# Two-layer graph network on one core: the first aggregation as seven products of 256 cubed, and the bias work moved behind the branch

## The chip, the cores and the metric

The kernel runs on one core of one Trainium2 chip. The metric is the device time of one execution in microseconds (us), from the first instruction to the last; runs of before and after are compared on the same chip. Five engines work in parallel, each through its own queue in order: PE (TensorE, matmuls), DVE (VectorE), ACT (ScalarE), POOL (GpSimd) and SP (which only issues DMAs).

## What is computed

The input x has 32 batches of 512 rows and 512 columns in fp32; adj is one 512 x 512 matrix for all of them. In short:

```python
h = relu(layernorm(x))
x = x + (adj @ h) @ W0 + b0                      # layer 0, per batch
h = relu(layernorm(x))
q, k, v = h @ Wq + bq, h @ Wk + bk, h @ Wv + bv   # 8 heads of 64
s = q @ k.T / 8 + (1 - adj) * -1e9
x = x + softmax(s) @ v @ Wo + bo                  # layer 1
```

The mask term has the size of 1e9 times a difference of adj, so a row's softmax puts all its weight on the column where adj has the row's maximum, as long as the scores are small against the gap. Then attention is a gather of rows: layer 1 becomes x + rows of (h @ Wv @ Wo + bv @ Wo + bo), and only those rows have to be computed that some row points to.

## The kernel before, in words

The function `gnn_two_layers` has two parts: work ahead of a branch (lines 72 to 308), and the branch (L310 on), which picks one of three paths by a number computed on the chip, the flag. On this input the path taken is `single_path` with room for 336 rows (its products are 168 wide).

**Ahead of the branch.** Everything stands in an order written out by hand, with no scheduler, so a line's place is its place in its engine's queue. The steps, in this order:

- Loads on SP and ACT (L88 to L97): Wv, Wo, adj, x of batch 0, Wq, Wk, W0, x of batch 1.
- Wv is transposed on PE (`turn`), and Wvo = Wv @ Wo is formed by `fold` (L149) in seven products of 256 cubed (Strassen's scheme in Winograd's form). Three PSUM banks `mm0` to `mm2` take the products; ACT copies or DVE adds them into `wvo`. The operand sums are made by `sum_a` and `sum_b` (L324 to L345), one DVE instruction each.
- The LayerNorm of batch 0 in two halves of two 128-row chunks (`norms[0]`, `norms[1]`). A half has four steps: `stats` (DVE, L359 and L360), `power` (DVE L365 and POOL L366), `offset` (DVE L369) and `relu` (ACT L377). The class `NormAct` does the same with statistics on ACT (L389; two passes with a running sum) and its own small steps at L397, L398 and L401.
- `peaks` (L156, L157): for each chunk of adj the row's eight largest values and the mask of the largest. `transposed` makes adjT on PE and copies it on ACT (L118).
- Five loads issued by POOL (L198, L200): bv, bq, bk as columns, b0 and bo as rows.
- The aggregation adj @ h of batch 0 (L270), as four groups of four 512-wide matmuls. Between them stand small products: the counts of used columns (L261, L264), the squared norms of Wq, bq, Wk, bk (L265, from ACT's `squares`, L240 and L241), the bias row bv @ Wo (L267, from the four `bias_part`s of DVE, L161 and L163) and the decision (L269).
- `decide` (L244 to L253) compares the least gap between a row's two largest values with a bound on the scores. L292 writes the flag.
- While PE finishes: two sums of Wvo, the addition of b0 to batch 0 (L298), the ReLU of batch 1, the index of each row's maximum (L304) and the bias column `cvo_c` (L305 and L308).

**Behind the branch.** `single_path` walks over the batches. In each round PE gets the layer 0 of batch b, the aggregation of batch b + 1, and the layer 1 of batch b - 1 (for b = 0: `layer0_rows`, L577, four groups of four 512-wide matmuls, and the aggregation of batch 1). Each of the three is a `product` of seven pieces of four matmuls (L451), with three to four PSUM banks taking turns; its pieces are p1, p5, u2, c11, c22, c12, c21. After each piece its bank is read by `take` (L488, L490, L498, L501, L508): c22, u2 and c21 continue in the bank of p1, c12 in that of p5, so a product that is added onto a bank waits for the read before it. All else is hung between the pieces: `put(batch, step, f)` puts a function into one of 21 steps of a round, steps 0 to 6 with the first product, 7 to 13 with the second and 14 to 20 with the third; in a step the functions come in the order of their `put`s, ahead of the `take`. In round 0, steps 3 to 6 are joined.

In round 0 the statistics of batch 0's second LayerNorm and of batch 2's first run on ACT (`NormAct`, eight pairs of L389). Steps 12 and 13 hold the remaining sums of W0 (L343, L345) and of Wvo (L331, L333).

Of the kernel before, what the change touches and what calls it, by code (L numbers as in the profile page):

```python
# [8 lines left out]
F32 = mybir.dt.float32  # L9
# [3 lines left out]
ALU = mybir.AluOpType  # L13
# [4 lines left out]
P = 128  # L18
HD = 64
EPS = 1e-5  # L20
NEG = 1e9
# [4 lines left out]
def gnn_two_layers(ctx: ExitStack, tc: tile.TileContext, x, adj, w0, b0, wq, bq, wk, bk, wv, bv, wo, bo, out):  # L26
# [22 lines left out]
    def big(name):  # L49
# [10 lines left out]
    before = keep.tile([P, C + 1], F32, name="before")  # L60
    idx = keep.tile([P, C, 8], U32, name="idx")
# [5 lines left out]
                wvo_t=wvo_t, cvo=cvo, cvo_c=cvo_c, b0_r=b0_r, used=used, before=before, idx=idx, ident=ident, ones=ones, mhalf=mhalf)  # L67
# [4 lines left out]
    with ExitStack() as tmp, tc.manual_schedule():  # L72
# [4 lines left out]
        part = look.tile([P, D], F32, name="part")  # L77
        wt = [look.tile([P, DC, D], F32, name=f"wt{i}") for i in range(2)]
        bt = [look.tile([P, DC], F32, name=f"bt{i}") for i in range(2)]
        bv_c = look.tile([P, DC], F32, name="bv_c")  # L80
# [71 lines left out]
        norms = [Norm(nc, small, mhalf, xs[0], hs[0], [0, 1]), Norm(nc, small, mhalf, xs[0], hs[0], [2, 3])]  # L152
# [5 lines left out]

        def bias_part(j):
            if j == 0:  # L160
                nc.vector.tensor_scalar_mul(part, wo_s[:, 0, :], bv_c[:, 0:1])  # L161
            else:
                nc.vector.scalar_tensor_tensor(part, wo_s[:, j, :], bv_c[:, j:j + 1], part, op0=ALU.mult, op1=ALU.add)  # L163
# [22 lines left out]
        nc.scalar.copy(blk(wvo, 1, 1), v)  # L186
        fold(u, wvT_t[:, 1], wo_t[:, 1], False)
        nc.scalar.copy(blk(wvo, 0, 1), u)
        peaks(0)
# [3 lines left out]
        norms[1].stats(0)  # L193
        norms[0].offset()
        norms[1].stats(1)
        norms[1].power()
# [6 lines left out]
        fold(u, wvT_t[:, 2], wo_t[:, 2], False)  # L203
        peaks(1)
        norms[1].offset()
        nc.vector.tensor_add(blk(wvo, 1, 1), u, blk(wvo, 1, 1))
# [3 lines left out]
        norms[0].relu(0)  # L210
        norms[0].relu(1)
        peaks(2)
        nc.vector.tensor_add(blk(wvo, 0, 1), v, blk(wvo, 0, 1))
        fold(u, blk(wvT, 1, 1), wo_t[:, 3], False)
        nc.scalar.copy(blk(wvo, 1, 0), u)
        norms[1].relu(0)
        norms[1].relu(1)
        peaks(3)

        both = look.tile([P, N], F32, name="both")  # L220
        nc.vector.tensor_add(both, sel[:, 0, :], sel[:, 1, :])
        for c in range(2, C):
            nc.vector.tensor_add(both, both, sel[:, c, :])  # L223

        tops = look.tile([P, C, 2], F32, name="tops")
        nc.vector.tensor_scalar(tops, top[:, :, 0:2], 1.0, NEG, op0=ALU.subtract, op1=ALU.mult)
        gap = look.tile([P, C], F32, name="gap")
        nc.vector.tensor_sub(gap, tops[:, :, 0], tops[:, :, 1])
        least = look.tile([P, 1], F32, name="least")
        nc.vector.tensor_reduce(least, gap, AX.X, ALU.min)  # L230
        for j in range(DC):
            bias_part(j)
# [22 lines left out]
        bias = corner(0).rearrange("p c q -> p (c q)")  # L255
        for d in range(DC):
            ps = bank((2, 1, 0, 2)[d]).rearrange("p a n -> p (a n)")
            for m in range(C):
                if d == 1 and m == 2:
                    for i in range(C):  # L260
                        nc.tensor.matmul(few[:, 0, i:i + 1], both[:, i * P:(i + 1) * P], ones[:, 0:1],  # L261
                                         start=True, stop=True)
                if d == 2 and m == 1:
                    nc.tensor.matmul(many[:, 0, :], ones, used, start=True, stop=True)  # L264
                    nc.tensor.matmul(many[:, 1, :], ones, sums, start=True, stop=True)  # L265
                if d == 2 and m == 3:
                    nc.tensor.matmul(bias, ones, part, start=True, stop=True)  # L267
                if d == 3 and m == 1:
                    nc.tensor.matmul(few[0:1, 1, 0:1], sure, ones[:, 0:1], start=True, stop=True)  # L269
                nc.tensor.matmul(ps, hs[0][:, m, d * P:(d + 1) * P], adjT[:, m, :], start=(m == 0), stop=(m == C - 1))  # L270
            if d == 0:
                squares(0)
            nc.scalar.copy(yT[:, d, :], ps)
            if d == 0:
                squares(1)
                for i in range(4):
                    sum_b(nc, adjT_s, adjT, i)
            if d == 1:
                nc.vector.tensor_scalar_min(used, few[:, 0, :], 1.0)
                if B > 1:  # L280
                    norms.append(NormAct(nc, small, mhalf, xs[1], hs[1], range(C)))
                    for c in range(C):
                        norms[2].stats(c)
                for i in range(2):
                    sum_b(nc, w0_t, w0_s, i)
            if d == 2:
                decide()
                nc.vector.memset(before[:, 0:1], 0.0)
                for m in range(1, C + 1):
                    nc.vector.tensor_add(before[:, m:m + 1], before[:, m - 1:m], many[:, 0, m - 1:m])  # L290
                nc.vector.tensor_add(cvo, bias, cvo)
        nc.vector.tensor_copy(flag, few[0:1, 1, 0:1])  # L292
        for i in range(2):
            sum_a(nc, wvo_t, wvo, i)
        if B > 1:
            norms[2].power()
# [755 lines left out]
```

## Time and profile before

| | us |
|---|---|
| time, median of 3 runs | 1081.98 (1081.93 to 1082.1) |
| the profiled execution's own time | 1081.54 |
| its span, first to last instruction | 1079.7 |
| PE busy | 1066.3 (99% of the span) |
| DVE busy | 898.7 (83%) |
| POOL busy | 447.1 (41%) |
| ACT busy | 376.2 (35%) |
| first aggregation, first matmul of L270 | 22.92 |
| flag written (L292) | 37.20 |
| first matmul behind the branch (L577) | 40.51 |
| first matmul of layer 0 of batch 1 | 67.98 |

The profile names an instruction by the line of the kernel it was issued from, the engine, the operation and "out<-in" by the names of the tiles. An fp32 matmul shows as two records. In a timeline a row is: start in us from the span's start, duration, engine, line, operation; in brackets the idle time of that engine ahead of it and who released it. In the chain that ended last, each piece was released by the one before it. The granted clock of PE was 0.999 throughout.

### The profile page before, as it was taken

How to read it: one execution, taken by the hardware profiler on the slowest of the kernel's cores; microseconds unless marked ns; L12 is line 12 of the kernel's file. 1: busy time of each engine (PE TensorE's matmuls, PEld its weight loads, DVE VectorE, ACT ScalarE, POOL GpSimd, SP SyncE). 2: the span in 40 equal slices, each digit the busy share in tenths (PEclk: the TensorE clock that was granted, in tenths of full speed). 3: DMA queues.
4: the chain of work that ended last, by engine and by line, in shares of the span. 5: the costliest groups of instructions: out<-in, count | busy, mean ns of one | idle time of the engine just before them, and what ended most of it. 6: DMA issues, size and time to landing. Idle time of an engine off the chain costs nothing.

```text
span 1079.7 us, 16014 instructions
## 1 busy us (share of the span) xinstructions
PE 1066.3 (99%) x5448; PEld 946.2 (88%) x5448; DVE 898.7 (83%) x1837; ACT 376.2 (35%) x709; POOL 447.1 (41%) x522
## 2 busy tenths in 40 slices
PE   9999999999999999999999999999999999999996
PEld 7478989999998999988999988999998999998993
DVE  6868888888888888888888888888888888888874
ACT  4744323334422324322323432323432323432331
POOL 2024554343554343554343454443454434355413
PEclk9999999999999999999999999999999999999999
DMA  9154666657776666767666767666776666766538
GB/s 330 40 92 145 183 184 160 157 169 197 186 185 158 165 168 187 193 174 183 148 169 184 199 170 195 143 168 175 205 187 183 148 157 180 199 180 165 133 106 272
DMA packets 162700, 186.92 MB, mean 173 GB/s; under 512 B 15024, under 2 KB 102832, under 8 KB 162608
## 3 DMA queue, kind: packets, MB, share of 16 engines
q1 hardware_dynamic: 132592, 116.73, 36.8%
q0 software_dynamic: 27968, 66.61, 27.4%
q10 hardware_dynamic: 2048, 2.46, 0.7%
q8 instruction: 45, 0.74, 0.3%
q14 instruction: 47, 0.39, 0.1%
HBM read 96.28 MB, written 89.46 MB: 172 GB/s over the span
## 4 chain that ended last, share of the span: by engine, by line
PE 93%; DVE 3%; DMA 2%; issue 1%; POOL 1%; ACTq 0%; ACT 0%; POOLq 0%; DVEq 0%
PE mm L451 91%; PE mm L577 1%; DMA x<-in_L_gnn_Wv_dram 1%; PE mm L270 1%; DMA yT<-z,place 1%; DMA z<-hc 0%; POOL hs L589 0%; DVE top L156 0%; DVE part L163 0%; DVE hc L656 0%; DVE st L359 0%; POOL rstd L398 0%; DVE sel L157 0%; DVE both L223 0%; POOL yT L674 0%
## 5 line engine op out<-in xcount | busy, mean ns | idle before, releaser
L665 POOL DMA_INDIRECT x<-z,place x116 | 182.8, 1576 | 351.3 <-issue 194.3
L490 ACT COPY yT<-mm 128x512 f32<-128x512 f32 x124 | 71.9, 580 | 541.9 <-PE mm L451 538.8
L508 DVE TENSOR_TENSOR x<-mm,x 128x512 f32<-128x512 f32 x217 | 149.8, 690 | 86.9 <-PE mm L451 86.9
L377 ACT ACTIVATE h<-x,off,rstd 128x512 f32<-128x512 f32 x256 | 194.5, 807 | 39.9 <-DVE off L369 35.8
L366 POOL TENSOR_TENSOR rstd<-ve,mhalf 128x2 f32<-128x2 f32 (+1 forms) x93 | 102.5, 1102 | 200.0 <-DVE ve L365 200.0
L451 PE MATMUL mm<-w_t,sel 128*128 128x256 f32 x744 | 171.0, 379 | 1.2 <-DVE x L508 1.2
L451 PE MATMUL mm<-adjT_s,h0s 128*128 128x256 f32 x744 | 171.0, 379 | 0.9 <-ACT yT L490 0.9
L359 DVE BATCH_NORM_STATS2 st<-x 128x6 f32<-128x512 f32 x244 | 163.4, 670 | 1.1
L451 PEld LDWEIGHTS mm<-w_t,sel 128*128 128x128 f32 x744 | 141.2, 190 | 20.8 <-DVE x L508 1.6
L451 PEld LDWEIGHTS mm<-adjT_s,h0s 128*128 128x128 f32 x744 | 141.2, 190 | 20.6 <-ACT yT L490 1.5
L589 POOL DMA_INDIRECT hs<-h,dest x124 | 133.2, 1074 | 23.6 <-issue 22.4
L451 PE MATMUL mm<-w_s,yT 128*128 128x256 f32 x496 | 117.2, 379 | 0.0
L451 PE MATMUL mm<-adjT,h 128*128 128x256 f32 x496 | 117.2, 379 | 0.0
L451 PE MATMUL mm<-hTs,wvo_t 128*128 128x168 f32 x720 | 112.4, 306 | 0.0
L501 ACT ACTIVATE zs<-mm,cvo_c 128x168 f32<-128x168 f32 x240 | 83.1, 397 | 75.0 <-PE mm L451 75.0
L451 PEld LDWEIGHTS mm<-adjT,h 128*128 128x128 f32 x496 | 94.2, 190 | 13.2 <-ACT h L389 0.2
L451 PEld LDWEIGHTS mm<-hTs,wvo_t 128*128 128x128 f32 x720 | 105.5, 190 | 0.0
L451 PEld LDWEIGHTS mm<-w_s,yT 128*128 128x128 f32 x496 | 92.9, 190 | 11.3
L557 DVE TENSOR_TENSOR x<-x,b_r 128x512 f32<-128x512 f32 x124 | 84.0, 677 | 0.0
L451 PE MATMUL mm<-hT,wvo 128*128 128x168 f32 x480 | 78.2, 306 | 0.0
L451 PEld LDWEIGHTS mm<-hT,wvo 128*128 128x128 f32 x480 | 72.7, 190 | 1.6
L488 DVE TENSOR_TENSOR yT<-mm,yT 128x512 f32<-128x512 f32 x93 | 64.0, 688 | 9.4 <-PE mm L451 4.9
(181 smaller groups left out, 1313.3 us busy)
## 6 DMA issues: line engine op xcount, KB each, us to landing
out_dram<-x SPq DMA_DIRECT2D x124, 256.0 KB, 4.7
x<-in_x_dram SPq DMA_DIRECT2D x120, 256.0 KB, 4.9
hc<-hs SPq DMA_DIRECT2D x124, 176.0 KB, 3.1
z<-zr SPq DMA_DIRECT2D x120, 96.0 KB, 2.0
z<-zr SPq DMA_DIRECT2D x120, 80.0 KB, 1.9
hs<-h,dest POOLq DMA_INDIRECT x124, 6.0
x<-z,place POOLq DMA_INDIRECT x116, 5.8
adj_s<-in_adj_dram SPq DMA_DIRECT2D x2, 512.0 KB, 5.8
```

Of the source, the lines that this page charges most:

```text
L270: nc.tensor.matmul(ps, hs[0][:, m, d * P:(d + 1) * P], adjT[:, m, :], start=(m == 0), stop=(m == C - 1))
L359: self.nc.vector.bn_stats(st, self.src[:, self.chunks[i], :])
L366: self.nc.gpsimd.tensor_tensor(self.rstd, ve, self.mhalf[:, 0:n], ALU.pow)
L377: self.nc.scalar.activation(dst, src, AF.Relu, bias=self.off[:, i:i + 1], scale=self.rstd[:, i:i + 1])
L451: nc.tensor.matmul(bank[:, m, 0:half], lhs[:, k, m * P:(m + 1) * P], rhs[:, k, :], start=(first and m == 0 and k == 0), stop=(k == 1), ski ...
L488: nc.vector.tensor_add(dst, bank, dst)
L490: nc.scalar.copy(dst, bank)
L501: nc.scalar.activation(dst[:, m, :], bank[:, m, :], AF.Identity, bias=cvo_c[:, 2 * i + m:2 * i + m + 1])
L508: nc.vector.tensor_add(dst, bank, dst)
L557: nc.vector.tensor_add(X[b][:, c, :], X[b][:, c, :], b0_r)
L589: stored = nc.gpsimd.indirect_dma_start(out=HS[b], out_offset=bass.IndirectOffsetOnAxis(ap=dest[:, i:i + 1], axis=0), in_=H1[b][:, i, :], ...
L665: nc.gpsimd.indirect_dma_start(out=X[b][:, c, :], out_offset=None, in_=Z[b], in_offset=bass.IndirectOffsetOnAxis(ap=place[:, c:c + 1], axi ...
```

## The change

- The aggregation of batch 0 ahead of the branch is done by a new helper `gemm` in seven products of 256 cubed, like all later ones. It needs four sums of h (`sum_a` into `wvT_t`, which is free by then) and four sums of adjT (`sum_b`, in the kernel before made between the groups). Three of the products are added to yT by DVE, four copied by ACT.
- The statistics of chunks 2 and 3 of batch 0 go to ACT (`NormAct`), and the order of powers, offsets, ReLUs, peaks and POOL's loads is changed with them.
- The bias row goes behind the branch: its parts to steps 9 and 10 of round 0, its product and addition to step 12. The bias column goes to step 6 of round 1.
- The sums of W0 (2 and 3) go from step 12 to step 8 of round 0, those of Wvo (2 and 3) from step 13 of round 0 to steps 5 and 6 of round 1. The sums 0 and 1 of W0 go behind the flag.
- In round 0 the second half of batch 0's second LayerNorm has its statistics on DVE, not on ACT.
- The small products of the decision stand behind the fifth, sixth and seventh product; L290's additions stand ahead of the flag as before.

```diff
-        norms = [Norm(nc, small, mhalf, xs[0], hs[0], [0, 1]), Norm(nc, small, mhalf, xs[0], hs[0], [2, 3])]
+        norms = [kind(nc, small, mhalf, xs[0], hs[0], [i, i + 1]) for i, kind in ((0, Norm), (2, NormAct))]
...
         nc.scalar.copy(blk(wvo, 1, 1), v)
+        norms[1].stats(0)
         fold(u, wvT_t[:, 1], wo_t[:, 1], False)
         nc.scalar.copy(blk(wvo, 0, 1), u)
+        norms[1].stats(1)
         peaks(0)
         for n in (0, 1):
             norms[0].stats(n)
         norms[0].power()
-        norms[1].stats(0)
-        norms[0].offset()
-        norms[1].stats(1)
-        norms[1].power()
         for t, d in ((bv_c, bv), (bt[0], bq), (bt[1], bk)):
             nc.gpsimd.dma_start(t, d.rearrange("(c p) -> p c", p=P))
...
         fold(u, wvT_t[:, 2], wo_t[:, 2], False)
+        norms[0].offset()
+        nc.vector.tensor_add(blk(wvo, 1, 1), u, blk(wvo, 1, 1))
+        norms[1].power()
         peaks(1)
         norms[1].offset()
-        nc.vector.tensor_add(blk(wvo, 1, 1), u, blk(wvo, 1, 1))
+        norms[0].relu(0)
+        norms[0].relu(1)
         next(flips)
         next(flips)
         fold(v, wvT_t[:, 3], wo_blk(1, 1), False)
-        norms[0].relu(0)
-        norms[0].relu(1)
+        norms[1].relu(0)
+        norms[1].relu(1)
         peaks(2)
+        for i in (0, 1):
+            sum_b(nc, adjT_s, adjT, i)
         nc.vector.tensor_add(blk(wvo, 0, 1), v, blk(wvo, 0, 1))
...
+        gemm(u, blk(h, 0, 0), blk(adjT, 0, 0), True)
+        squares(0)
+        nc.scalar.copy(blk(yT, 0, 0), u)
+        squares(1)
+        for i in (0, 1):
+            sum_a(nc, h_t, h, i)
+        gemm(w, blk(h, 1, 0), blk(adjT, 1, 0), True)
+        sum_a(nc, h_t, h, 2)
+        sum_b(nc, adjT_s, adjT, 2)
+        nc.vector.tensor_add(blk(yT, 0, 0), w, blk(yT, 0, 0))
+        gemm(u, h_t[:, 1], adjT_s[:, 1], False)
+        nc.scalar.copy(blk(yT, 0, 1), u)
+        peaks(3)
+        gemm(v, h_t[:, 0], adjT_s[:, 0], True)
+        nc.scalar.copy(blk(yT, 1, 1), v)
+        if B > 1:
+            norms.append(NormAct(nc, small, mhalf, xs[1], hs[1], range(C)))
+            for c in range(C - 1):
+                norms[2].stats(c)
...
+        gemm(u, h_t[:, 2], adjT_s[:, 2], False)
+        for i in range(C):
+            nc.tensor.matmul(few[:, 0, i:i + 1], both[:, i * P:(i + 1) * P], ones[:, 0:1], start=True, stop=True)
...
+        gemm(v, h_t[:, 3], blk(adjT, 1, 1), False)
+        nc.tensor.matmul(many[:, 0, :], ones, used, start=True, stop=True)
+        nc.tensor.matmul(many[:, 1, :], ones, sums, start=True, stop=True)
+        decide()
+        nc.vector.tensor_add(blk(yT, 0, 1), v, blk(yT, 0, 1))
+        gemm(u, blk(h, 1, 1), adjT_s[:, 3], False)
+        nc.tensor.matmul(few[0:1, 1, 0:1], sure, ones[:, 0:1], start=True, stop=True)
+        nc.scalar.copy(blk(yT, 1, 0), u)
+        if B > 1:
+            norms[2].stats(C - 1)
+        nc.vector.memset(before[:, 0:1], 0.0)
+        for m in range(1, C + 1):
+            nc.vector.tensor_add(before[:, m:m + 1], before[:, m - 1:m], many[:, 0, m - 1:m])
         nc.vector.tensor_copy(flag, few[0:1, 1, 0:1])
         for i in range(2):
             sum_a(nc, wvo_t, wvo, i)
+        for i in range(2):
+            sum_b(nc, w0_t, w0_s, i)
...
-                halves = [norm(X[b], H1[b], [2 * i, 2 * i + 1], Norm if b > 0 else NormAct) for i in range(2)]
+                halves = [norm(X[b], H1[b], [2 * i, 2 * i + 1], Norm if b > 0 or i == 1 else NormAct) for i in range(2)]
...
                 for i in (2, 3):
-                    put(0, 12, lambda b, i: sum_b(nc, w0_t, w0_s, i), i)
-                    put(0, 13, lambda b, i: sum_a(nc, wvo_t, wvo, i), i)
+                    put(0, 8, lambda b, i: sum_b(nc, w0_t, w0_s, i), i)
+                for j in range(DC):
+                    put(0, 9 + j // 2, lambda b, j: bias_part(j), j)
+                put(0, 12, lambda b: bias_row())
...
+                for i in (2, 3):
+                    put(1, 3 + i, lambda b, i: sum_a(nc, wvo_t, wvo, i), i)
+                put(1, 6, lambda b: bias_column())
```

The removed lines of the old aggregation are L255 to L291 of the kernel before; the functions `bias_part`, `bias_row` and `bias_column` have the instructions of L161, L163, L267, L291, L305 and L308, unchanged.

## The prediction

> **What bounds the kernel now.** I read the page first: TensorE is busy 99% of the span and the chain that ended last lies on it for 93%.
>
> ```profile
> span 1079.7 us, 16014 instructions
> ...
> PE   1066.3 (99%) x5448; PEld 946.2 (88%) x5448; DVE 898.7 (83%) x1837; ACT 376.2 (35%) x709; POOL 447.1 (41%) x522
> ...
> PE 93%; DVE 3%; DMA 2%; issue 1%; POOL 1%; ACTq 0%; ACT 0%; POOLq 0%; DVEq 0%
> ```
>
> Second came the chain in order of time: from 100.89 us on it is one unbroken piece of PE, 953.68 us long, so the change can only act in the first 101 us and in what they hand on. Third, the timeline of PE up to there (start, time, what, and in brackets the idle time before it with its releaser):
>
> ```profile
> 22.92 5.31 PE L270 MATMUL mm<-adjT,h 128*128 128x512 f32 x12
> ...
> 34.16 1.02 PE L267 MATMUL pt<-part,ones 128*128 128x512 f32 x2
> ...
> 40.51 7.10 PE L577 MATMUL mm<-w_s,yT 128*128 128x512 f32 x16 [0.72 <-ACT yT L273]
> ...
> 59.24 1.99 PE L451 MATMUL mm<-adjT_s,h0s 128*128 128x256 f32 x8 [0.86 <-ACT yT L490]
> ...
> 62.80 1.89 PE L451 MATMUL mm<-adjT_s,h0s 128*128 128x256 f32 x8
> 64.52 1.89 PE L451 MATMUL mm<-adjT,h0s 128*128 128x256 f32 x8
> ...
> 72.79 1.99 PE L451 MATMUL mm<-w_t,sel 128*128 128x256 f32 x8 [1.20 <-DVE x L508]
> ```
>
> The last rows give the price of a product of 256 cubed: 64.52 - 62.80 = 1.72 us. The 16 records of L577 take 6.94 us until L525 starts, so a 512-wide matmul is two records, 0.87 us. Fourth, the timelines of DVE, POOL and SP, for the steps that move:
>
> ```profile
> 37.05 0.15 DVE L292 CAST flag<-few 1x1 int32<-1x1 f32 x1 [1.14 <-PE few L269]
> ...
> 43.75 0.67 DVE L305 TENSOR_TENSOR part<-cvo,ident 128x512 f32<-128x512 f32 x1
> 44.45 0.69 DVE L308 TENSOR_REDUCE cvo_c<-part 128x4 f32<-128x512 f32 x1
> ...
> 80.73 0.70 DVE L359 BATCH_NORM_STATS2 st<-x 128x6 f32<-128x512 f32 x1
> ...
> 100.34 0.49 DVE L498 TENSOR_TENSOR zs<-mm,zs 128x336 f32<-128x336 f32 x1
> ```
>
> From 80.73 to 100.83 DVE idles only 1.4 us (0.81 waiting for POOL's power, 0.17 and 0.42 for PE). At 100.89 PE waits for that L498. So there DVE, not PE, hands the time on.
>
> [...] the trace has 0.68 to 0.69 us, and such instructions follow each other every 0.60 us, which I use. [...] the flag is written at 37.20, SP's first DMA behind the branch starts at 37.92, 0.72 us. [...]
>
> **The change, part by part.** I laid out each engine's queue in its new order, with durations from the rows above and each instruction behind what it reads.
>
> *Ahead of the aggregation.* The statistics of chunks 2 and 3 of batch 0 go from DVE to ACT, two pairs of 1.46 us (from the L389 rows). One pair now stands before the copy of the second folding bank, so the next fold waits about 0.35 us at 16.2; but the addition into wvo now stands ahead of the peaks on DVE and PE's 0.36 us wait at 21.09 is gone. Nil: the aggregation starts at 22.9 as before. Moved past POOL's five loads: the second power. They take 3.63 us (19.99 to 23.62), started now at 18.0, so the power is done at 22.4. Behind it DVE has the offset, one pair of peaks (1.14), two adjT sums (1.3) and the addition that empties a folding bank: 25.7. The second product writes that bank and is ready at 24.6, so PE waits 1.1 us, a new wait. Its bounds are 0 (if the power were served between the loads) and 1.1. And if the small loads bq and bk land later than 5.6 us after issue (they now run beside the big loads), the squares on ACT hold the copy of the first product and up to 1 us more is lost. I take zero for that.
>
> *The aggregation.* Removed: 16 matmuls of 0.863 = 13.8 us. Added: 28 of 0.432 = 12.1 us. The bias matmul (0.86) leaves. The count products (0.80 + 0.44 + 0.11) stay. From 22.9: 12.1 + 1.35 + 1.1 = 37.4 us as PE's end, against 39.8 before. The operand sums (seven more DVE instructions, 4.2 us) are costed at nothing: four bias parts (2.7), the bias addition (0.6) and two bn_stats pairs (1.6) leave DVE's queue there, 4.9 us. If they didn't cover it, each sum in front of its product would cost its 0.60. But now the flag comes last: the decision waits for products behind the sixth of seven, and a yT addition, the memset and four dependent additions of 0.20 stand before the flag's cast. It ends at 38.45, 1.25 us later than before, and PE has nothing queued. With SP's 0.72 us PE restarts at 39.15 instead of 40.51: lead 1.36 us. Bounds of this restart: 0.35 us (DVE's own gap at the branch, 45.14 to 45.48) and 3.3 us (all that the old row could have hidden, 37.20 to 40.51).
>
> *Behind the branch to the first wait.* Layer 0 of batch 0 and two products are equal in both: PE is ready for the third at 56.8. DVE does the same amount between flag and branch (two w0 sums for the bias column) but starts 1.2 us later, so ACT's statistics start at 47.9, not 46.93. ACT has six pairs instead of eight: 8.8 + copy 0.6, done at 57.25. PE waits 0.45, restarting at 57.3 against 59.24: lead 1.94. The bias matmul comes back (0.86), waiting for nothing since its four parts end at about 61.7: lead 1.1 at 66.8.
>
> *The 1.20 us wait at 72.79.* DVE had two w0 sums and two wvo sums in front of the four sums of yT and the first addition of x. All four are moved away. From the bias product (ends 65.1) DVE needs 0.7 + 0.65 + 2.7 + 0.7 to that addition, 69.8; PE needs it at 70.25. The wait is gone and the lead is 2.5 us. Slack 0.4.
>
> *The giving back.* One wvo sum and the bias column have been put behind the statistics of batch 1: 0.60 + 0.70 + 0.65 = 1.95 us more in the saturated stretch of DVE that begins at 80.73. It begins 2.5 us earlier, but ends only 2.5 - 1.95 + 0.59 (its two waits for PE, which vanish) = 1.15 us earlier. PE, ahead by 2.5, waits for DVE and ACT at about 86, 90 and 99 us, 1.3 us in all. Behind 101 us PE has no wait to lose, and loads, stores and gathers move along with it.
>
> *Sum.* The profiled execution: 1079.7 + 1.84 around the span = 1081.54 us; minus 1.15 gives 1080.4. The runs' median is 1081.98, so 1080.8 on that footing.
>
> **Rivals.** A difference under 0.2% (2.2 us) is about what a measurement of this kernel can tell from none.
>
> *Nothing is given back.* The 2.5 us stay: 1079.5, faster. For it: PE is the 99% engine. Against it: the L498 row and DVE's density from 80 to 101. It would need the three instructions to fall into idle time, of which there is 0.8 us.
>
> *The exposed branch decides: slower.* In the new order every engine learns the path only when PE is empty. If PE's restart takes 3.3 us instead of 0.72, 2.6 us are lost, of which the 0.45 us wait at 57 takes up some: 1080.8 + 2.1 = 1082.9. Slower than before from a restart of about 2.3 us on; beyond 0.2% only from 4.6 us. [...] Against it: SP's 0.72.
>
> *Small loads late.* 1 us in ACT's squares: 1081.8, no change in effect.
>
> **Numbers.** My case 66%, 1080.2 to 1081.6; nothing given back 12%; exposed branch 12%; late loads 10%. The range reaches into the first rival and half of the second: 1079.6 to 1082.3. Faster by over 0.2% (below 1079.8): most of the first rival, 11%. Slower by over 0.2% (above 1084.1): a part of the second, 6%. The rest, 83%.
>
> **What would show it.** Right: PE's first behind-branch matmul near 39.2 us with a wait for the flag before it; a PE wait of about 1 us near 25 us; no wait at 70; waits near 86, 90 and 99 us with DVE or ACT as releaser; the third aggregation about 1.1 us earlier than 102.0. Wrong: a restart past 40.5, a wait behind 101 us, or PE without waits from 80 to 101. A time under 1079.6 or over 1082.3 would refute the sum.

## The result, and where the time went

The kernel after takes 1084.58 us (median of 20 runs, 1083.31 to 1086.81), the kernel before 1082.24 us on the same chip: ratio 1.0020, 95% interval 1.0014 to 1.0026, or 1.5 to 2.8 us slower. On another chip the same comparison gave 1.0015 (1.0008 to 1.0021). The forecast was 1080.8 us with a range up to 1082.3.

The profiled execution took 1085.0 us; its page answers to the lines shown of before:

```profile
span 1083.3 us, 16074 instructions
...
PE 1066.4 (98%) x5472; PEld 950.6 (88%) x5472; DVE 903.5 (83%) x1844; ACT 376.0 (35%) x709; POOL 447.4 (41%) x522
...
PE 91%; DVE 3%; DMA 2%; issue 1%; POOL 1%; ACT 1%; SPq 0%; ACTq 0%; POOLq 0%; DVEq 0%
```

PE is as busy as before (1066.4 against 1066.3 us) in a span 3.6 us longer: nothing in sum is saved on PE, and the rest is waiting. One sum hides two: PE's work fell, and part of it ran at half speed. The timeline of PE (start, duration, what; in brackets the idle time before it):

```profile
22.57 1.89 PE L238 MATMUL mm<-adjT,h 128*128 128x256 f32 x8
25.67 1.97 PE L238 MATMUL mm<-adjT,h 128*128 128x256 f32 x8 [1.22 <-DVE wvo L210]
28.42 5.45 PE L238 MATMUL mm<-adjT_s,x 128*128 128x256 f32 x24 [0.78 <-ACT yT L246]
...
38.59 0.19 PE L286 MATMUL few<-ones,sure 128*1 128x1 f32 x2
40.92 8.80 PE L595 MATMUL mm<-w_s,yT 128*128 128x512 f32 x16 [2.14 <-ACT h L388]
...
71.54 3.62 PE L450 MATMUL mm<-w_t,sel 128*128 128x256 f32 x16
...
102.33 1.41 PE L450 MATMUL mm<-hTs,wvo 128*128 128x168 f32 x8 [0.84 <-DVE zs L497]
103.58 1.89 PE L450 MATMUL mm<-w_s,yT 128*128 128x256 f32 x8
...
123.31 1.99 PE L450 MATMUL mm<-adjT_s,h0s 128*128 128x256 f32 x8 [0.57 <-ACT yT L489]
```

Two waits in the aggregation, then 2.14 us without work at the branch, where the kernel before had 0.72. Behind it the 16 records of L595 take 8.80 us instead of 7.10. The table by stretches says why; the third column from the right is PE's granted clock:

```profile
41.00:42.00 1.00, 1.00 (x3) 0.52 (x4) 0.96 (x3) 0.00 (x0) 0.00 (x0) 1.00 0.02 8
42.00:43.00 1.00, 1.00 (x3) 0.32 (x2) 1.00 (x3) 0.00 (x0) 0.30 (x1) 0.66 0.76 295
43.00:44.00 1.00, 1.00 (x3) 0.41 (x2) 1.00 (x3) 0.00 (x0) 1.00 (x1) 0.50 1.06 408
44.00:45.00 1.00, 1.00 (x3) 0.48 (x2) 1.00 (x2) 0.00 (x0) 0.57 (x2) 0.50 0.94 334
45.00:46.00 1.00, 1.00 (x2) 0.37 (x2) 1.00 (x6) 0.78 (x2) 0.00 (x0) 0.63 0.01 4
46.00:47.00 1.00, 1.00 (x4) 0.40 (x3) 1.00 (x3) 1.00 (x3) 0.00 (x0) 1.00 0.00 0
```

From 42.33 to 45.74 us, 3.41 us long, the chip gave PE half its clock: 1.7 us of work lost. (The 0.999 given for before is a mean: there the clock was full from 5.85 to 1077.63 us, PE's last matmul ended at 1072.27, and the clock was half from 1077.63 to the end.) The stretch at half clock follows 2.14 us without work on PE; whether it comes from them is what e1, e2 and e4 ask.

The other half is on DVE. It writes the flag at 39.89 instead of 37.20, and does its first instruction behind the branch at 48.24 instead of 45.48:

```profile
39.75 0.14 DVE L293 CAST flag<-few 1x1 int32<-1x1 f32 x1
48.24 0.69 DVE L326 TENSOR_TENSOR h0s<-h 128x512 f32<-128x512 f32 x1 [0.40 <-ACT h L376]
```

The chain that ended last, in order of time (start, length, what), shows the links that are new:

```profile
18.82 6.86 DMA bt<-in_L_gnn_bq_dram
26.00 1.89 ACT wt L221 x2
28.42 5.45 PE mm L238 x24
...
107.00 2.06 SPq L679
...
109.11 2.07 DMA z<-zr
...
118.22 1.53 POOL x L683
119.75 0.77 POOL rstd L365
...
122.78 0.48 ACT yT L489
...
123.31 196.93 PE mm L450 x1024
```

The first new link is a load of 2 KB, bq, which takes 6.86 us from issue to landing and holds the squares and with them the copy of the first product. And behind 102 us, where the kernel before had one piece of PE 953 us long, there is a second late passage: a store of z whose issue took 2.06 us and its landing 2.07, four gathers, a power, two ReLUs and a copy.

Against before, PE is 1.83 us behind at layer 0 of batch 1 (69.81 against 67.98), 0.37 at the third aggregation (81.90 against 81.53), 1.45 at the next round (103.58 against 102.13), 2.55 a round later and 2.7 at the last round. Of the rest of the 3.6, 0.3 us are lost up to PE's last matmul and 0.6 behind it, in the last gathers and stores.

### The profile page after: what moved, and what is told of

Same layout as the page of the kernel before. It is cut to its first block, busy times and chain, and to the rows that moved or that the text cites. A ratio compares the mean times of both kernels' runs of the same rounds, so it can differ in the third digit from the quotient of the medians.

```text
span 1083.3 us, 16074 instructions
## 1 busy us (share of the span) xinstructions
PE 1066.4 (98%) x5472; PEld 950.6 (88%) x5472; DVE 903.5 (83%) x1844; ACT 376.0 (35%) x709; POOL 447.4 (41%) x522
## 4 chain that ended last, share of the span: by engine, by line
PE 91%; DVE 3%; DMA 2%; issue 1%; POOL 1%; ACT 1%; SPq 0%; ACTq 0%; POOLq 0%; DVEq 0%
PE mm L450 88%; PE mm L595 1%; PE mm L238 1%; DMA bt<-in_L_gnn_bq_dram 1%; DMA yT<-z,place 1%; DMA x<-in_L_gnn_Wv_dram 1%; DVE st L358 1%; POOL x L683 0%; DMA z<-hc 0%; SPq L679 0%; POOL rstd L365 0%; DVE x L575 0%; DMA z<-zr 0%; DVE hT L656 0%; DVE x L507 0%
## 5 line engine op out<-in xcount | busy, mean ns | idle before, releaser
L365 POOL TENSOR_TENSOR rstd<-ve,mhalf 128x2 f32<-128x2 f32 (+1 forms) x93 | 103.4, 1112 | 196.3 <-DVE ve L364 196.3
```

Of the source, the lines that this page charges most:

```text
L365: self.nc.gpsimd.tensor_tensor(self.rstd, ve, self.mhalf[:, 0:n], ALU.pow)
```

## The experiments

In the table, "DVE" is the start of its first instruction behind the branch, "PE" that of its first matmul there, "half" whether the granted clock fell to 0.5 behind the gap at the branch, "next" the start of PE's next round, "power" the time that POOL took for the power of 128 x 4 ahead of that start, the same instruction in all runs (see e8); all in us from one profiled execution. The ratio is to before on the same chip, with its 95% interval.

| run | DVE | PE | half | next | power | ratio |
|---|---|---|---|---|---|---|
| before | 45.48 | 40.51 | no | 102.13 | 1.41 | 1 |
| after | 48.24 | 40.92 | yes | 103.58 | 1.41 | 1.0020 (1.0014 to 1.0026) |
| e8 after again | 48.31 | 40.96 | yes | 104.64 | 3.22 | 1.0015 (1.0008 to 1.0021) |
| e1 keep busy | 48.03 | 40.71 | no | 103.26 | 3.22 | 1.0009 (0.9999 to 1.0019) |
| e14 busy, same fetch | 47.80 | 40.44 | no | 103.06 | 3.22 | 1.0015 (1.0007 to 1.0023) |
| e2 flag first | 48.16 | 40.06 | no | 102.37 | 1.41 | 1.0024 (1.0014 to 1.0034) |
| e5 column early | 48.23 | 40.91 | yes | 102.49 | 1.41 | 1.0012 (1.0005 to 1.0018) |
| e9 fetch later | 48.02 | 40.67 | no | 102.23 | 1.41 | 1.0017 (1.0010 to 1.0024) |
| e13 relieved only | 45.74 | 40.54 | no | 101.50 | 1.41 | 1.0009 (1.0001 to 1.0017) |
| e3 power first | 45.44 | 38.08 | yes | 100.75 | 1.41 | 1.0000 (0.9991 to 1.0008) |
| e6 both waits | 45.85 | 37.75 | no | 101.08 | 3.21 | 0.9991 (0.9983 to 1.0000) |
| e7 all | 43.63 | 37.66 | no | 97.54 | 1.41 | 0.9971 (0.9960 to 0.9981) |
| e12 all again | 43.54 | 37.57 | no | 98.47 | 3.22 | 0.9970 (0.9961 to 0.9979) |
| e10 all, fetch later | 43.39 | 37.42 | no | 97.31 | 1.41 | 0.9970 (0.9961 to 0.9978) |
| e4 before, exposed | 45.12 | 42.47 | yes | 105.76 | 3.22 | 1.0013 (1.0007 to 1.0020) |
| e11 before, fetch early | 50.43 | 45.47 | no | 107.08 | 1.41 | 1.0045 (1.0032 to 1.0058) |

e8 is the kernel after once more, for comparison on one chip:

> The kernel after, unchanged, so that the others of this call can be compared with it on the same chip. Both theories: 2.3 us (0.2%) over the kernel before.

It gave 1.4 us over before; its next round came 1.06 us later than in the first trace. One instruction made the difference, the power on POOL, first in after, then in e8, with the offset on DVE that needs it:

```profile
98.44 1.41 POOL L365 TENSOR_TENSOR rstd<-ve,mhalf 128x4 f32<-128x4 f32 x1 [4.93 <-DVE ve L364]
100.70 0.15 DVE L368 SCALAR_TENSOR_TENSOR off<-mv,rstd 128x4 f32<-128x4 f32 x1
```

```profile
98.49 3.22 POOL L365 TENSOR_TENSOR rstd<-ve,mhalf 128x4 f32<-128x4 f32 x1 [4.93 <-DVE ve L364]
101.74 0.16 DVE L368 SCALAR_TENSOR_TENSOR off<-mv,rstd 128x4 f32<-128x4 f32 x1 [0.94 <-POOL rstd L365]
```

DVE lost 0.94 us, and PE's wait at 102 us was 1.86 instead of 0.84. The kernel is the same, so this is no effect of any edit, and starts of the next round can only be compared between traces with a like power. The long one stands in e8, e1, e14, e6, e12 and e4.

### The gap of PE and the half clock: e1, e2, e4, e14

```diff
         nc.tensor.matmul(few[0:1, 1, 0:1], sure, ones[:, 0:1], start=True, stop=True)
+        idle = corner(3)
+        for i in range(16):
+            nc.tensor.transpose(idle[:, i % 4, :], ident, ident)
         nc.scalar.copy(blk(yT, 1, 0), u)
```

> The kernel after, with 16 transposes of the identity into an unused PSUM bank behind the decision product, so that PE works on while the flag travels (about 16 x 0.13 = 2.1 us, as long as the gap of 2.14 us). Nothing else is changed; the transposes write nothing that is read. Clock theory (the gap of PE makes the chip halve PE's clock for one window of 3.41 us, 1.7 us lost): the granted clock stays at 1.0 behind the branch, the 16 records of L595 take 7.0 us instead of 8.80, and the time falls by about 1.7 us to 1082.9 (at least 1.0 us, since some runs of the kernel after had no such window). Branch theory (what is slow behind the branch is the restart itself, fetching of instructions or operands): no change, 1084.6, records of L595 still 8.8 us.

The gap fell to 0.24 us, the window at the branch was gone, the records of L598 (L595 of after) took 7.11 us. But PE then waited 1.86 us for DVE at 102 and got its half-clock window there, from 103.3; about 1 us of that wait is the long power. Against e8, which had the long power too, the next round came 1.38 us earlier. Time: 1.6 us over before, interval -0.1 to 2.1 by the ratio; the gain of 1.7 is not confirmed.

```diff
+        nc.vector.tensor_copy(flag, few[0:1, 1, 0:1])
         nc.vector.memset(before[:, 0:1], 0.0)
         for m in range(1, C + 1):
             nc.vector.tensor_add(before[:, m:m + 1], before[:, m - 1:m], many[:, 0, m - 1:m])
-        nc.vector.tensor_copy(flag, few[0:1, 1, 0:1])
```

> The kernel after, with the cast that writes the flag put ahead of the memset and the four additions of the row numbering, which wait for each other. The flag is then written at about 38.95 instead of 39.89 and PE restarts at 39.98 (1.03 us behind the flag): gap 1.2 us instead of 2.14. If the gap's length alone counts: 0.94 us less, 1083.6. If in addition the clock drop needs a gap longer than 1.2 us: 0.94 + 1.7 us less, 1081.9. If DVE behind the branch bounds (its work is the same and ends at the same time): no change, 1084.6.

PE did what the second theory says at the branch, and the time did not fall, as the third says. The timeline of PE in this run:

```profile
40.06 7.11 PE L595 MATMUL mm<-w_s,yT 128*128 128x512 f32 x16 [1.22 <-ACT h L388]
...
59.00 1.99 PE L450 MATMUL mm<-adjT_s,h0s 128*128 128x256 f32 x8 [1.07 <-ACT yT L489]
```

Gap 1.22 us, full clock, and then 1.07 us of waiting for a copy on ACT: ACT's statistics start behind DVE's passing of the branch, and that stayed at 48.16. So the 0.86 us that PE won at the branch were worth nothing at the next round: e2 began it at 102.37, e9 (below), which had no window either and PE 0.61 us later, at 102.23. The full clock was worth 1.2 us there, against 103.58 in after. But the time is 2.9 us over before. In this trace PE fell back against before by 1.2 us in round 1, by 1.1 in round 12, and by 0.8 in the last round; its end came another 1.0 later. Only the first has a cause found (the fetches, below).

e4 is the kernel before with its flag made late and nothing else changed:

```diff
-                if d == 3 and m == 1:
-                    nc.tensor.matmul(few[0:1, 1, 0:1], sure, ones[:, 0:1], start=True, stop=True)
                 nc.tensor.matmul(ps, hs[0][:, m, d * P:(d + 1) * P], adjT[:, m, :], start=(m == 0), stop=(m == C - 1))
+                if d == 3 and m == 3:
+                    nc.tensor.matmul(few[0:1, 1, 0:1], sure, ones[:, 0:1], start=True, stop=True)
```

The cast of the flag goes behind the additions of b0, the offset and the first index search.

> The kernel before, with the branch exposed as in the kernel after, and nothing else: the decision product stands behind the last matmul of the aggregation, and the cast of the flag behind the additions of b0, the offset and the first index search (the same DVE instructions, later flag). PE empties at 39.9 and restarts at about 41.8, a gap of about 1.9 us instead of 0.72. Clock theory: a half-clock window follows the gap in the kernel before too, 1.3 + 1.7 us lost, less the wait of 0.86 us at the second aggregation: 1084.3. Rival (half clock comes from the seven products or from something else in the new order, not from the gap): granted clock 1.0 behind the branch, 0.5 us lost, 1082.7.

The gap came out longer than meant, so that the times forecast don't apply (2.1 us over before, 0.8 to 2.2 by the ratio), and the half clock came with it:

```profile
42.47 8.77 PE L580 MATMUL mm<-w_s,yT 128*128 128x512 f32 x16 [2.93 <-ACT h L380]
```

So it belongs to the gap, not to the seven products. Over all traces, behind the first 20 us: gaps of 1.83 to 2.93 us, at the branch or at 102 us, were followed by a window in six cases (after, e8, e5, e3, e4; e1 at 102) and not in five (e9, e13; e6, e8 and e14 at 102); no gap up to 1.37 us was.

The traces show what decides. In each, the clock is half again at the end, where PE has finished (in after from 1079.98 us on; its last matmul ended at 1075.24). Where there is a window as well, the two starts lie a whole number of steps apart, each of 3.413 us as the window of after is long: 1037.65 us or 304 steps in after, e8, e3 and e4, 303 steps in e5, 286 in e1. So in these traces the clock changes on a grid of 3.413 us, which falls differently in each execution. Laid back from the end, the grid tells how much of a gap fell into one stretch. In after, e8, e5 and e4 it was 2.0 to 2.9 us, and the next stretch was at half clock. In e9, e13, e14 and e8 at 102 us a boundary cut the gap, the greatest part was 1.1 to 1.5 us, and the clock stayed full. At 1.86 to 1.96 us both occur: e1 and e3 got the window, e6 didn't. The boundary in these traces is thus near 1.9 idle us of 3.41, as an estimate, since the ends of matmuls are modelled. So a gap of about 2.1 us can bring the half clock (after) or not (e9).

Between traces with a like power, the window is worth 1.2 to 1.6 us at the next round: 103.58 in after against 102.23 and 102.37 in e9 and e2; 104.64 in e8 against 103.26 and 103.06 in e1 and e14. What it is worth in the time is harder to say. In the runs of after with a mean granted clock of at least 0.998 (9 of 20) the mean time is 1083.80 us, in those of at most 0.996 (7) it is 1085.72; in e8 1084.03 (11 of 21) and 1085.73 (5). But the mean clock also counts the half clock at the end (2.1 us in the trace of before, 3.3 in that of after), and the kernel before, on the chip of e1 to e4, shows a like step between 0.999 (12 runs, 1082.55 us) and 0.997 (7 runs, 1084.65). So this is no price of the window.

e14 is e1's edit together with the one of e9 (below), so that the blocks of instructions (see the fetches below) should stay where after has them.

> The kernel after with PE kept busy by 16 transposes while the flag travels, and with the short warm-up (12 instructions instead of 40), so that PE's instruction blocks are fetched where they are in after (28 instructions fewer, 32 more); DVE passes the branch at 48.2 as in after. PE theory (the half clock behind the gap costs 1.2 us or more where it occurs, in about half of the executions): no half-clock window at the branch, the mean time 0.6 to 1 us below after, and runs with a granted clock under 0.997 rare. DVE theory: what PE wins here it waits for DVE at 59 and 101 us, time as after, 0.15 to 0.2% over before.

Only one of 13 runs had a granted clock under 0.997, against 12 of 41 in after and e8 and none of 159 of before: the windows look rarer, as the PE theory has it. The mean is 1084.32 us, 1.3 over the mean of before on its chip, where after and e8 stood 2.4 and 1.7 over theirs; but the intervals overlap, and 0.15% by the ratio is what the DVE theory names. PE waited 0.36 us for ACT at 59, 0.15 at 88 and 1.86 for DVE at 102; of the last, about 1 us is the long power and not the edit. Undecided between the two.

### What makes the flag late, and DVE with it: e3, e6

In the diff of e3 the removed lines of the loads are left out.

```diff
+        norms[1].power()
+        for t, d in ((bv_c, bv), (bt[0], bq), (bt[1], bk)):
+            nc.gpsimd.dma_start(t, d.rearrange("(c p) -> p c", p=P))
...
         norms[0].offset()
         nc.vector.tensor_add(blk(wvo, 1, 1), u, blk(wvo, 1, 1))
-        norms[1].power()
...
-        squares(0)
         nc.scalar.copy(blk(yT, 0, 0), u)
-        squares(1)
+        squares(0)
...
         nc.scalar.copy(blk(yT, 0, 1), u)
+        squares(1)
```

> The kernel after, with the second power of batch 0's LayerNorm ahead of POOL's five loads and ahead of the first offset on DVE, and ACT's squares behind the copies into yT. Theory of the two waits: PE's waits of 1.22 us (for the addition into wvo) and 0.78 us (for the copy of the first product) both vanish, PE comes to the decision 2.0 us earlier, the flag at about 37.9 and the restart at 38.9, and everything up to the third aggregation moves along: 1082.6, the half clock behind the branch still there. Rival: the squares are now the late ones, and PE waits for them at the sums product instead, up to 2 us, or DVE is the bound up to the decision: less than 0.7 us gained, 1084.

Both waits vanish, PE restarts at 38.08 and DVE passes the branch at 45.44, 2.8 us earlier than in after; the next round begins 2.83 us earlier, the half clock still there. That is 0.8 us more than the two waits: without them the first five products take 1.73 us each. The time equals that of before, so 1.4 to 2.3 us below after. The first theory holds: bq's squares ahead of a copy and POOL's power behind five loads made the new order late. Both were moved at once, so their shares in the time aren't separated.

e6 has the edits of e3 and e2 together.

> The second power ahead of POOL's loads and the squares behind the copies, as in the run with the power first, and the flag's cast ahead of the four additions, as in the run with the flag first. Gap theory: PE idles about 1.2 us at the branch, no half-clock window behind it, PE restarts at 37.2. But what DVE does between flag and branch ends no earlier than in the run with the power first (45.0), and ACT starts its statistics behind that: so PE waits about 1 us for ACT's copy at the second aggregation, and the gain over the run with the power first is about 1.2 us at 101 us. Time: 3.2 us less than the kernel after. Rival (PE's lead ahead of 60 us is worth nothing since DVE is dense from 44 to 100 us): as the run with the power first, 2.0 us less than after.

The time is 0.7 us below before (1.8 below to level), with an interval that overlaps that of e3. It is 2.1 us less than after (e8) by the medians and 2.6 by the ratios, between the two theories. The wait at the second aggregation came as expected (1.07 us). The next round did not: it began 0.33 us later than in e3 instead of 1.2 earlier. This trace has the long power and that of e3 the short; with the 1 us of e8 taken off, it would be some 0.7 us earlier.

### DVE: e5, e13, e7, e12

```diff
...
+                put(1, 1, lambda b: bias_column(0))
+                put(1, 3, lambda b: bias_column(1))
-                put(1, 6, lambda b: bias_column())
```

> The kernel after, with the two instructions of the bias column moved from step 6 of round 1 to steps 1 and 3, where DVE idles 0.44 us four times while it waits for PE. Theory (the lead is given back between 81 and 102 us because 1.95 us of DVE work were put into DVE's dense stretch there): PE's wait of 0.84 us at 101.5 shrinks to nothing, the next round starts 0.9 us earlier, 0.9 us less than the kernel after. Rival (the stretch is bounded by the arrival of rows and by ACT, or what is won is lost again at the gathers of z behind it): next round earlier by less than 0.3 us, or no difference in time.

The wait for L497 fell from 0.84 to 0.27 us, as in before, and the next round came 1.09 earlier, with PE's restart and half clock as in after: work of DVE between 81 and 102 us is handed on to PE. Between the medians it is 0.6 us (1083.79 against 1084.41 for e8 on the same chip), within the intervals.

```diff
+        nc.vector.max_index(idx[:, 0, :], top[:, 0, :], adj_s[:, 0, :])
         nc.vector.tensor_scalar_min(used, few[:, 0, :], 1.0)
...
+        nc.vector.max_index(idx[:, 1, :], top[:, 1, :], adj_s[:, 1, :])
         decide()
...
-        for i in range(2):
-            sum_a(nc, wvo_t, wvo, i)
...
+            if B > 1 and c == 1:
+                norms[2].offset()
...
+                for i in (0, 1):
+                    put(0, 8, lambda b, i: sum_a(nc, wvo_t, wvo, i), i)
```

> The kernel after with DVE alone relieved ahead of the branch: two index searches stand where DVE waits for PE, the first two sums of Wvo go to step 8 of round 0, batch 1's offset stands behind two of the additions of b0. PE's part is left as it is: both waits in the aggregation, the flag at 39.9, the restart at 40.9. DVE begins behind the branch at about 45.7 instead of 48.24. DVE theory (the time follows DVE's passing of the branch, since DVE is dense from there to 103 us): the next round starts 1 us earlier where PE has had a half-clock window, 2 us where not, and the time is 1 to 2 us below after, 0.1% or less over before. PE theory (PE's late restart and its half clock set the time): as after, 0.15 to 0.2% over before.

DVE passes the branch at 45.74, no window came in this trace (gap 1.83), and the next round starts at 101.50, 0.73 us ahead of e9, which had no window either. In time it is 1.0 over before, 0.1 to 1.8 by the ratio; in the seven runs with a granted clock of 0.998 or more the mean is 1083.15, 0.27 over the mean of before in such runs on that chip, against 1.14 in e8. That suggests about 1 us for DVE's lateness and the rest for the half clock, which e13 has left in; but it compares a selection of runs on two chips, and by the ratios the intervals of e13 and e8 overlap.

e7 puts e3, e2, e5 and e13 together.

> As the run with both waits, and DVE relieved ahead of the branch and at 81 to 102 us: two of the four index searches stand where DVE waits for PE ahead of the branch, the first two sums of Wvo go to step 8 of round 0, the offset of batch 1 stands behind two of the additions of b0, and the bias column stands at steps 1 and 3 of round 1. DVE then reaches the branch at 42.4 instead of 45.0. Theory (DVE is what hands the time on from the branch to 102 us): next round starts at about 97 us, 5 us ahead of the kernel before, and the time is 4 to 5 us below before, 6 to 7 below after. Rival (what is won ahead of 102 us is lost behind it, as in the run with the power first): next round at 97 us, but the time not more than 2 us below before.

PE starts its next round at 97.54, 4.59 us ahead of before, and the time is 2.9 us below before (2.1 to 4.3): faster than both kernels, less than the 4 to 5 us expected, more than the rival's 2. The step from e6 to e7 is 2.2 us in time, with intervals that don't meet: that is what the edits to DVE's order are worth.

e12 is e7 once more:

> The run with everything moved, once more, on the chip of this call: 0.3% below before, as the first time; round 1 again about 32.7 us with the fetch at 3.7 us.

The same ratio again. The next round came 0.93 us later than in e7, since POOL's power of 128 x 4 (L365) took 3.22 us here and 1.41 there; DVE waited for it.

### The fetches of instructions: e9, e10, e11

From the next round to the last, the kernel after loses 1.25 us against before, e3 1.25 and e7 1.6, nearly all of it in single rounds. In most of these a packet of kind "instruction" lies amid the stores of z. The DMA view of after, from the first store of z to the end of the last issue, 104.2 to 109.6 us (queue, packets, MB, share):

```profile
q1 hardware_dynamic: 1123, 0.53, 39.5%
q8 instruction: 1, 0.02, 1.7%
```

The same stretch of before, 102.7 to 108.1 us:

```profile
q1 hardware_dynamic: 1536, 0.72, 51.3%
q0 software_dynamic: 64, 0.00, 0.9%
```

All 1536 packets of z are through there, in after only 1123: one packet of kind "instruction", 16 KB, took 1.48 us (from 107.2) in front of them. In before that block came 7.3 us into the round, behind the stores, and took 1.41 us. Over rounds 1 to 28 of all sixteen traces, 59 have such a packet between 3.4 and 4.8 us into the round, and 45 of these take over 32.2 us, where an undisturbed round takes 32.15; of the other 389 rounds 26 do, 15 of them round 12, whose delay has no cause found. So the packet delays most rounds that it hits, not all. The trace of after has 45 such packets of 16 KB on q8 and 10944 records of PE and its weight loads: one packet for about 243 of them. The author's estimate was that these blocks are PE's instructions, so that they move against the work when PE gets more or fewer of them ahead of it. e9 shortens PE's warm-up in instructions, not in time:

```diff
-        for i in range(20):
-            nc.tensor.transpose(idle[:, i % 4, :], ident, ident)
+        for i in range(2):
+            nc.tensor.matmul(idle, ident, ident.unsqueeze(1).broadcast_to([P, 4, P]), start=True, stop=True)
+        for i in range(2):
+            nc.tensor.transpose(idle[:, i, :], ident, ident)
```

> The kernel after, with the 20 warm-up transposes at PE's start (L162) replaced by two 512-wide matmuls and two transposes of the identity into the same unused bank: about the same 4 us of PE, but 12 instructions instead of 40, so every 16 KB block of PE's instruction stream is fetched 28 instructions, some 3 us, later against the work. Fetch theory (the block fetched 3.6 us into round 1 stands in front of the stores of z, which land 1.6 us late, and the gathers, POOL's power and ACT's copies behind them): the fetch comes at 6.6, the last z lands at 6.0 instead of 7.6, the gathers start at 7.0 instead of 9.0, round 1 takes 32.2 us instead of 33.26, and over all rounds 1.2 us are won. Rival (the stores are late for another reason, such as loads of x or the look-ups beside them): stores and gathers as in after, time as after.

In the trace the theory holds. POOL's gathers of after and of e9, whose next round begins at 102.23:

```profile
112.59 1.60 POOL L683 DMA_INDIRECT x<-z,place  x1 [7.01 <-issue]
```

```profile
109.64 1.60 POOL L685 DMA_INDIRECT x<-z,place  x1 [5.41 <-issue]
```

That is 9.0 and 7.4 us into the round. The block now comes 7.6 us into it instead of 3.6, with 28 instructions fewer on PE; the round takes 32.15 us instead of 33.26, and from there to the last round PE loses 0.2 us instead of 1.25. But the time is 1.7 us over before, as after on the two other chips; the 1.2 us are not found there. The profiled execution was the fastest of the 18, and had no half-clock window, so it doesn't stand for the others.

e10 has e9's warm-up in the kernel of e7.

> The same edit of the warm-up in the run with everything moved. Fetch theory: round 1 takes 32.2 us instead of 32.7, all rounds together lose 0.8 us instead of 2.1, time 1 us below the run with everything moved. Rival: as that run.

PE loses 0.6 us behind the next round instead of 1.2 to 1.6. The median is 1079.0 us against 1079.52 of e12 on the same chip, the ratios are alike.

```diff
-        for i in range(20):
-            nc.tensor.transpose(idle[:, i % 4, :], ident, ident)
+        for i in range(18):
+            nc.tensor.matmul(idle[:, i % 4, 0:64], ident, ident[:, 0:64], start=True, stop=True)
```

> The kernel before, with the 20 warm-up transposes replaced by 18 matmuls of 64 columns: about the same PE time, but 72 instructions instead of 40, so that the fetch comes some 3.7 us earlier against the work. Fetch theory: the block that came 7.3 us into round 1, behind the stores, now comes at about 3.6, amid them; the gathers start at 8.4 to 9.0 instead of 7.0 and round 1 takes 0.5 to 1.1 us longer; over all rounds about 1 us slower than before. Rival (the late stores come from the new order of the work, not from the fetch): round 1 stays at 32.15 us and the time is that of before.

The kernel before with the block moved amid its stores by 32 more instructions on PE, 4.0 us into the round instead of 7.3: its gathers start 8.35 us into the round instead of 7.0 and the round takes 32.61 us instead of 32.15. The late stores come with the fetch, whatever the order of the work. The time says nothing: the 36 records of 64 columns took 7.94 us where the 20 of 128 columns had taken 4.53, 0.22 us each against 0.23; the clock rose from half to full at 13.75 us instead of 5.85 (in before the transposes ahead of that start every 0.21 us, those behind it every 0.11), and the next round began 4.95 us later.

So the mechanism is shown in profiled executions, at 0.3 to 1.2 us where it hits round 1; what it costs in runs without a profile stays open (under about 1 us by e9 and e10).

## Why the prediction was wrong, step by step

- *Ahead of the aggregation.* Right: the first product starts at 22.57 (forecast 22.9), the fold waits 0.23 us (0.35), the second product 1.22 us (1.1) for the addition behind POOL's power.
- *The price of a sum on DVE.* Right: an fp32 tensor_tensor of 128 x 512 took 0.68 to 0.69 us, and the next could start 0.60 us behind it, in before (66.39, 66.99, 67.59) and in after (59.74, 60.34, 60.95).
- *The small loads.* Wrong: "I take zero for that" gave no reason for the zero. bq landed 6.86 us after issue instead of 5.6, and PE waited 0.78 us for the first product's copy. The rival that named it had 10%.
- *"It ends at 38.45" (the flag): the step that failed.* It was 39.89. Of the 1.44 us, 0.78 are that wait, 0.12 the first wait, and 0.75 the seven products, which took 12.85 us together instead of 12.1, those beside a wait or a small product 0.1 to 0.2 us longer each than the 1.73 used; the early start gave 0.33 back, and 0.1 is rounding and small products. e3 took both waits away and won 2.8 us at the next round and the whole loss in time. A restart past 40.5 was the prediction's own sign of being wrong; it was 40.92.
- *The restart.* 1.03 us behind the flag, not 0.72: 0.3 us short, inside the bounds given.
- *A term that was missing.* The gap was costed by its length, 0.7 us. Its 2.14 us halved PE's clock for 3.41 us, 1.7 us on PE. At the next round that is worth about 1.3 us (1.2 to 1.6 by the four pairs above). It comes in a part of the executions only, by where the grid falls; its share in the median time is not settled.
- *DVE "starts 1.2 us later".* It was 2.76 later at the branch, the flag's lateness in full (39.89 - 37.20 = 2.69). The forecast had seen that DVE hands the time on from 80 us, but not that it does so from the branch: in e2 PE's 0.86 us were gone by the next round.
- *The 1.20 us wait at 72.79.* Right: gone. (The lead of 2.5 us behind it is a slip of 0.2: the lead of 1.1 and the wait of 1.20 make 2.3.) *The giving back.* Right in size: from 81.9 to 103.58 PE lost 1.08 us (forecast 1.35), 0.84 of it waiting for L497 instead of in three waits at 86, 90 and 99 us, and e5 won 1.09 us back by moving the bias column.
- *"Behind 101 us PE has no wait to lose".* Wrong in the trace: 1.1 us lost in one round, 1.25 up to the last, when a fetch delayed the stores of z.
- *The sum.* Forecast for the next round 102.13 - 1.15 = 100.98; measured 103.58. Of the 2.60, about 1.3 are the half clock and 1.3 the later flag, by difference. e9 bears that out: it had no window, its flag was written at 39.67, 1.22 us behind the forecast's, and its next round came 1.25 us behind it. Up to there the rest of the forecast's sum held, in one trace. Of the rivals, the exposed branch was the right place at the wrong price, and it came together with the late loads; the chances treated them as exclusive.

What stays open: how DVE's lateness and the half clock divide the 1.4 to 2.3 us of the timed runs (e13 and e14 each took away only a part, with intervals that overlap), what delays the last round and the stores behind it by 0.9 us in the profile, why e2 was slower than its next round promised, and the fetches' share in time.

## What to carry to other kernels

When a branch, a flag or any hand-over is moved to where an engine has nothing queued, cost not only the wait but who else stands behind it: here DVE's work on the far side came later by the whole delay (2.76 us), and PE's clock halved for 3.41 us in six of the sixteen traces. Don't put a small load's reader, or a step that waits for a busy issuing queue, ahead of a copy that frees a bank: here the two together cost 2.83 us at the next round (e3). And a saving on the 99% engine is worth only what the next engine lets pass: with both waits gone and the flag early the time was 0.1% below before, and taking work off DVE at the branch and in its dense stretch made it 0.3%. Before a time in one trace is read as an edit's effect, look for an instruction that took another time in it: here one power on POOL moved the next round by 1 us.

## What the runs showed that was not expected

- In these traces a pause of PE of 1.83 us or more halved its clock for 3.41 us in six of eleven cases; none up to 1.37 us did. It went by the idle part of one stretch of a 3.413 us grid: 1.99 us and more always, 1.55 and less never.
- A 16 KB block of instructions took 1.0 to 1.6 us to transfer where it met round 1, and when it fell 3.6 to 4.6 us into that round, amid the stores of z, the gathers started at 8.2 to 9.1 us instead of 7.0 to 7.4.
- One and the same power on POOL (L365, 128 x 4) took 1.41 us in ten profiled executions and 3.22 us in six; after and e7 had the short one, their repeats e8 and e12 the long one, and a next round that started about 1 us later. No cause was found. Without knowing this, e1, e14 and e6 look 1 us worse at the next round than they are.
- 64-column fp32 matmuls in the warm-up took 0.22 us each, as long as the 128-column transposes of before there (0.23), and PE's clock rose at 13.75 us instead of 5.85.
